# Moving the turned sequences and the dense convolutions among the stages that run beside a scan

## The chip, the cores and the metric

One core of a Trainium2 chip runs the whole program in one launch. The engines are PE (TensorE: matmuls and, as PEld, their weight loads), DVE (VectorE), ACT (ScalarE), POOL (GpSimd) and SP (SyncE, which here issues every DMA). Each engine takes its instructions in the order in which the program gives them, so an instruction that waits holds back what stands behind it on the same engine. The metric is the device time of the launch in microseconds (us), the median of several runs. Beside it stands one execution under the hardware profiler, from which all durations below are taken.

## What is computed

Eight images of 64 x 64 positions with 192 channels pass through two layers. Cut to what matters, the second layer of the reference is

```
y = conv3x3(bn(xl)); y = conv3x3(relu(bn(y)))          # dense convolutions, 96 channels
xl_out = relu(conv1x1(relu(bn(y))))
xi = silu(depthwise3x3(in_proj(ln(xr))))               # 192 channels
xs4 = [x_hw, x_wh, flip(x_hw), flip(x_wh)]             # rows first, and turned: columns first
h = exp(d_t * A) * h + (d_t * u_t) * b_t;  y_t = h . c_t   # the scan, 4096 steps, 4 directions, 16 states
yv = ys[0] + flip(ys[2]) + turned back(ys[1] + flip(ys[3])) + D * xs4
xr_out = out_proj(ln(yv) * silu(z))
out = interleave(xl_out, xr_out) + x
```

The first layer is of the same family: a projection, a depthwise convolution, a state-space pass in chunks that is done with matmuls, and an MLP. The second layer's scan has no such form here and runs as true scans on DVE.

## The kernel before

The second layer's scan is the backbone. An image's scan is cut into 384 units (8 stretches of 1024 steps, 3 tiles of channels, 16 units in a tile), 3072 in all. In each unit SP fetches a tile `dA` (`fetch`, 6 units ahead), ACT takes its exponential (`decay`, L1450, 2 units ahead), PE spreads the input into `dB` (`spread`, L1458, one unit ahead), DVE weighs it (L1473) and scans it (L1480), POOL multiplies by C (L1482), and PE gathers the states of four units (L1500). A unit of the scan has two halves, and in each half the loop calls `beside.half()`.

`Beside` holds a list of stages: Python generators which, each time they are advanced, emit a few instructions and yield a cost, or None for "no more in this half". Each half adds a credit, `rate`, and takes stages' costs from it. `spread_over` sets `rate` when an image begins, from the sum of the stages' costs and the number of halves; a stage that has run in full once (`finish` in front of the first scan) is known by what it yielded, `conv_branch` and `scan_outputs` by numbers written out by hand. What is left when the next image's scan is about to begin, at unit 360 of 384, is emitted at one go by `beside.finish()`. The new image's stages begin at unit 362.

While image b - 1 is scanned, the stages for image b and for the scan of image b - 2 run, in this order:

- `conv0`, `ssd`, `mlp0`: the first layer of image b, whose output is `x1[b]`
- `conv_branch(b - 2)`: the dense convolutions (L895), with `scan_sums(b - 2)` as its side: the sum of the four directions
- `scan_outputs(b - 2)`: normalisation, gate and output projection
- `scan_inputs(b)`: normalisation, projection and depthwise convolution, which writes the sequences `us[b]`
- `transposed(b)`: reads the sequences back in quarters (`whole<-u`, L1114), turns each quarter on ACT into a tile `part` (L1124) and stores it (L1132)

A side is advanced by `cx.aside()` once in each half, up to its next None, in addition to the stage it belongs to; what it yields as cost is ignored. Stages 0 run alone in front of the first scan. During the last image's scan only `conv_branch(6)` with the sums of image 6, `scan_outputs(6)` and `conv_branch(7)` are left, and the sums and outputs of image 7 follow behind the scan (the tail).

SBUF for each stage comes from pools that are opened and closed like a stack; `us`, `ys` and `xns` lie in DRAM, each image's at an address of its own. Matmul results of side work rotate through four PSUM banks (`cx.one`).

Of the kernel before, what the change touches and what calls it, by code (L numbers as in the profile page):

```python
# [1 line left out]

# [7 lines left out]
F32 = mybir.dt.float32  # L10
# [6 lines left out]
HH = WW = 64  # L17
L = HH * WW
PW = WW + 2
C = 192  # L20
CH = C // 2
# [30 lines left out]
def wh(ap):  # L52

    return ap.rearrange("p (h w) -> p w h", h=HH)


def wh_to_hw(ap):

    return ap.rearrange("p (w h) -> p h w", w=WW)
# [16 lines left out]
class Shared:  # L76
# [5 lines left out]
    def __init__(self, tc):  # L82
        self.tc, self.nc, self.pin = tc, tc.nc, tc.keep_in_program_order
        self.k = {}
        self.singles = []
        self.side = None

    def one(self, name):

        self.singles.append(self.singles.pop(0))  # L90
        return self.singles[-1].tile([128, 512], F32, tag="n", name=name)

    def aside(self):

        for piece in self.side or ():
            if piece is None:
                return True
        self.side = None
        return False

# [189 lines left out]
def pause(n):  # L290

    for i in range(n):
        yield None
# [810 lines left out]
def transposed(cx, u):  # L1104

    nc, pin = cx.nc, cx.pin
    with cx.pool("t1") as tp:
        wholes = []
        for n, src in enumerate((u[0], u[2][0:64])):
            wholes.append(tp.tile([src.shape[0], L], F32, tag=f"whole{n}", name=f"whole{n}"))  # L1110

        def load(n, q):
            here = slice(q * L // 4, (q + 1) * L // 4)
            pin(nc.sync.dma_start(out=wholes[n][:, here], in_=(u[0], u[2][0:64])[n][:, here]))  # L1114

        for q in range(4):
            load(0, q)
            yield from pause(1 if q < 3 else 2)
        front = []
        for whole, dst in zip(wholes, (u[1], u[2][64:128])):  # L1120
            for q in range(4):
                w0 = q * WW // 4
                part = tp.tile([whole.shape[0], L // 4], F32, tag="part", name="part", bufs=4)
                pin(nc.scalar.copy(part.rearrange("p (w h) -> p w h", h=HH), wh(whole)[:, w0 : w0 + WW // 4, :]))  # L1124
                front.append((dst[:, q * L // 4 : (q + 1) * L // 4], part))
                if whole is wholes[0]:
                    load(1, q)
                if q % 2 == 1:
                    yield 1.0
                    yield None  # L1130
                if len(front) == 2:
                    pin(nc.sync.dma_start(out=front[0][0], in_=front.pop(0)[1]))  # L1132
        pin(nc.sync.dma_start(out=front[0][0], in_=front.pop(0)[1]))


def scan_sums(cx, y, u):

    nc, pin, k = cx.nc, cx.pin, cx.k

    def slots(n):  # L1140
        for i in range(n):
            yield 1.0
            yield None

    def cols(r, n):
        return slice(r * n, (r + 1) * n)

    with cx.pool("t2") as tp:

        for size, firsts, seconds, v, skip, eye in (  # L1150
            (128, [p[0] for p in y], [p[1] for p in y], u[0], k["skip_a"], k["ident"]),
            (64, [p[2][0:64] for p in y], [p[2][64:128] for p in y], u[2][0:64], k["skip_b"], k["twice"]),
        ):
            whole = tp.tile([128, L], F32, tag="whole", name="whole")
            for q in range(4):
                here = cols(q, L // 4)
                pin(nc.sync.dma_start(out=whole[:size, here], in_=seconds[0][:, here]))
                if size < 128:
                    pin(nc.sync.dma_start(out=whole[size:, here], in_=seconds[1][:, here]))
                yield from slots(1)  # L1160
            if size < 128:
                yield from slots(1)
            else:
                others = []
                for q in range(NB + 1):
                    if q < NB:
                        others.append(tp.tile([128, 512], F32, tag="p1", name="p1", bufs=2))
                        pin(nc.sync.dma_start(out=others[q], in_=seconds[1][:, cols(q, 512)]))
                    yield from slots(3 if q == 0 else 1)
                    if q > 0:  # L1170
                        here = cols(q - 1, 512)
                        pin(nc.gpsimd.tensor_add(whole[:, here], whole[:, here], others[q - 1]))

            def load(r):
                part = tp.tile([128, 512], F32, tag="part", name="part", bufs=3)
                pin(nc.sync.dma_start(out=part[:size], in_=firsts[0][:, cols(r, 512)]))
                vt = tp.tile([size, 512], F32, tag="vt", name="vt", bufs=2)
                pin(nc.sync.dma_start(out=vt, in_=v[:, cols(r, 512)]))
                if size < 128:
                    pin(nc.sync.dma_start(out=part[size:], in_=firsts[1][:, cols(r, 512)]))  # L1180
                    return part, [(eye, part), (skip, vt)]
                p1 = tp.tile([128, 512], F32, tag="p1", name="p1", bufs=2)
                pin(nc.sync.dma_start(out=p1, in_=firsts[1][:, cols(r, 512)]))
                return part, [(eye, part), (eye, p1), (skip, vt)]

            coming = load(0)
            yield from slots(4)
            for r in range(NB):
                (part, terms), coming = coming, load(r + 1) if r + 1 < NB else None
                yield from slots(1)  # L1190
                ps = cx.one("ps_sum")[:size]
                for i, (w, t) in enumerate(terms):
                    pin(nc.tensor.matmul(ps, lhsT=w, rhs=t, start=i == 0, stop=False))  # L1193
                rows = wh_to_hw(whole)[:, r * RB : (r + 1) * RB, :]
                pin(nc.tensor.matmul(ps.rearrange("p (h w) -> p h w", w=WW), lhsT=eye, rhs=rows, start=False, stop=True))
                yield 0.6 * len(terms)
                yield None
                pin(nc.scalar.copy(part[:size], ps))
                yield from slots(1)
                pin(nc.sync.dma_start(out=firsts[0][:, cols(r, 512)], in_=part[:size]))  # L1200
# [72 lines left out]
class Beside:  # L1273
# [14 lines left out]
    def half(self):  # L1288

        self.cx.aside()  # L1290
        self.credit = min(self.credit, self.rate) + self.rate
        while self.credit > 0.0 and self.stages:
            for cost in self.stages[0]:
                if cost is None:
                    return
                self.credit -= cost
                if self.credit <= 0.0:
                    return
            self.stages.pop(0)
# [287 lines left out]
def vision_mamba_pair_kernel(ctx: ExitStack, tc: tile.TileContext, x: bass.AP, p0: dict, p1: dict, out: bass.AP):  # L1587

    B = x.shape[0]
    cx = Shared(tc)  # L1590
# [3 lines left out]
    x1 = dp.tile([B, C, L], F32, tag="x1", name="x1")  # L1594
    cx.singles = [ctx.enter_context(tc.tile_pool(name="ps", bufs=4, space=PSUM))]
    setup(cx, cp, dp, p0, p1)
    us, ys, xns = {}, {}, {}

    def short(b):

        return x1[b].rearrange("(i g) l -> g i l", g=2)

    def sums(b):
        return scan_sums(cx, ys[b], us[b])

    def outputs(b):
        return scan_outputs(cx, ys[b][0], xns[b], short(b)[1], out[b][1])

    def branch(b, side=None):
        return conv_branch(cx, x1[b][0:CH], short(b)[0], out[b][0], side)  # L1610

    def stages(b):

        if b < B:
            us[b] = [d2.tile([128, L], F32, tag=f"u{t}", name=f"u{t}") for t in range(3)]
            ys[b] = [[d2.tile([128, L], F32, tag=f"y{g}{t}", name=f"y{g}{t}") for t in range(3)] for g in range(2)]
            xns[b] = d2.tile([CH, L], F32, tag="xn", name="xn")
            beside.add(conv0(cx, x[b]))
            beside.add(ssd(cx))
            beside.add(mlp0(cx, x[b], x1[b]))  # L1620
        if b > 1:
            beside.add(branch(b - 2, sums(b - 2)))
            beside.add(outputs(b - 2))
        if b == B:
            beside.add(branch(b - 1))
        if b < B:
            beside.add(scan_inputs(cx, x1[b][CH:C], xns[b], us[b]))
            beside.add(transposed(cx, us[b]))

    beside = Beside(cx)  # L1630
    with tc.tile_pool(name="ps_a", bufs=4, space=PSUM) as more:
        cx.singles.append(more)
        stages(0)
        beside.finish()
        beside.costs.update(conv_branch=190.0, scan_outputs=78.0)
        cx.singles.remove(more)

    def tail():
# [100 lines left out]
```

## Time and profile before

| what | us |
|---|---|
| median of 3 runs | 16441.98 (16431.81 to 16492.6) |
| profiled execution: span | 16436.7 |
| in front of the first scan unit | 902.0 |
| scan of image 0 | 1792.5 |
| scans of images 1 to 6 | 1970.2, 1989.4, 1983.3, 2000.9, 1984.0, 1983.7 |
| scan of image 7 | 1589.2 |
| behind the last scan | 241.6 |
| busy: PE, DVE, ACT, POOL | 13372.1, 12230.0, 10412.7, 10527.5 |

The times of the scans are differences between starts of the first L1480 of each image. A scan and its weighing take DVE 2344 ns and 1216 ns, 3.6 us together, so a scan that nothing holds up lasts 384 x 3.6 = 1382 us. No engine is busy all the time: the share of PE is 81% over the span, of DVE 74%, and the DMA engines' is 78.5%. Which of them sets the pace changes from stage to stage, and a share over the span does not tell it. That is why the prediction reads the profile by stages: from the unit in which a stage's first instruction is emitted to the unit of its last.

### The profile page before, as it was taken

How to read it: one execution, taken by the hardware profiler on the slowest of the kernel's cores; microseconds unless marked ns; L12 is line 12 of the kernel's file. 1: busy time of each engine (PE TensorE's matmuls, PEld its weight loads, DVE VectorE, ACT ScalarE, POOL GpSimd, SP SyncE). 2: the span in 40 equal slices, each digit the busy share in tenths (PEclk: the TensorE clock that was granted, in tenths of full speed). 3: DMA queues.
4: the chain of work that ended last, by engine and by line, in shares of the span. 5: the costliest groups of instructions: out<-in, count | busy, mean ns of one | idle time of the engine just before them, and what ended most of it. 6: DMA issues, size and time to landing. Idle time of an engine off the chain costs nothing.

```text
span 16436.7 us, 210821 instructions
## 1 busy us (share of the span) xinstructions
PE 13372.1 (81%) x69608; PEld 4636.5 (28%) x69608; DVE 12230.0 (74%) x9264; ACT 10412.7 (63%) x20023; POOL 10527.5 (64%) x5766
## 2 busy tenths in 40 slices
PE   8977887788877897878888788777898788878876
PEld 4423322332223321333223332233322333211111
DVE  2178887886878767887678876788767886778994
ACT  4466677665775757757576575766657666655654
POOL 3158766775668656686567765677656775566773
PEclk9987888789887897878888798887988779877766
DMA  3288888788887888878888778887778877888885
GB/s 89 84 218 195 210 205 225 190 204 208 204 219 187 205 205 207 209 191 204 208 208 207 198 196 198 217 205 197 204 193 221 198 202 205 193 227 200 211 204 137
DMA packets 1602582, 3241.31 MB, mean 197 GB/s; under 512 B 390152, under 2 KB 841368, under 8 KB 1601496
## 3 DMA queue, kind: packets, MB, share of 16 engines
q1 hardware_dynamic: 1601496, 3227.83, 78.5%
q8 instruction: 559, 9.16, 0.3%
q14 instruction: 527, 4.32, 0.1%
HBM read 2548.91 MB, written 678.18 MB: 196 GB/s over the span
## 4 chain that ended last, share of the span: by engine, by line
PE 30%; DMA 16%; DVE 14%; ACT 13%; POOL 7%; issue 5%; SPq 2%; DVEq 0%; ACTq 0%; POOLq 0%
DVE h L1480 9%; DMA dA<-dld 5%; PE acc L1500 5%; DVE dB L1473 4%; PE ps_c L895 4%; PE ps_cv L343 3%; POOL h L1482 3%; ACT dA L1450 3%; PE dB L1458 2%; DMA dus<-dud 2%; PE ps_sum L1193 1%; ACT L107 1%; PE ps_m L799 1%; PE ps_y L696 1%; ACT h L830 1%
## 5 line engine op out<-in xcount | busy, mean ns | idle before, releaser
L1482 POOL TENSOR_TENSOR h<-h,bc 128x1023 f32<-128x1023 f32 x3072 | 7228.8, 2354 | 4585.2 <-DVE h L1480 3895.8
L1480 DVE TENSOR_TENSOR_SCAN h<-dA,carry,dB 128x1024 f32<-128x1024 f32 x3072 | 7200.8, 2344 | 820.7 <-ACT dA L1450 257.6
L1473 DVE TENSOR_TENSOR dB<-dB,bc 128x1024 f32<-128x1024 f32 x3072 | 3736.3, 1216 | 1827.5 <-PE dB L1458 1823.9
L1450 ACT ACTIVATE dA<-dA,neg_a 128x1024 f32<-128x1024 f32 x3072 | 3512.9, 1144 | 29.3 <-DMA dA<-dld 24.1
L1500 PE MATMUL acc<-h,gather 128*32 128x512 f32 x12288 | 2364.1, 730 | 596.5 <-ACT h L1489 329.0
L1458 PE MATMUL dB<-dus,spread 24*128 24x512 bf16 x6144 | 1370.2, 435 | 664.5 <-DVE h L1480 620.1
L1505 ACT COPY y<-acc 128x512 f32<-128x512 f32 x1536 | 884.8, 576 | 750.3 <-PE acc L1500 677.4
L895 PE MATMUL ps_c<-p,conv_w 96*96 96x512 f32 x2304 | 1287.7, 685 | 37.9 <-ACT p L915 26.9
L1488 ACT COPY carry<-h 128x1 f32<-128x1 f32 x3072 | 584.2, 190 | 856.9 <-DVE h L1480 854.4
L1458 PEld LDWEIGHTS <-spread 24*128 24x128 bf16 x6144 | 308.0, 93 | 2837.2 <-issue 1395.5
L1489 ACT ACTIVATE h<-h,bc 128x1 f32<-128x1 f32 x3072 | 905.2, 295 | 143.3 <-ACT carry L1488 1.8
L696 PE MATMUL ps_y<-X,M 64*64 64x64 f32 x12288 | 605.6, 270 | 418.6 <-issue 232.7
L624 ACT ACTIVATE M<-ps_d,ln_dt 128x64 f32<-128x64 f32 x3072 | 669.1, 335 | 314.6 <-PE ps_d L630 304.6
L343 PE MATMUL ps_cv<-pad,diag 64*64 64x512 f32 x6912 | 841.0, 605 | 7.1 <-ACT y L1505 5.1
L1500 PEld LDWEIGHTS acc<-h,gather 128*32 128x32 f32 x12288 | 311.2, 117 | 1636.3 <-issue 1040.1
L107 ACT ACT_TABLE_LOAD x577 | 740.3, 1283 | 10.0
L696 PEld LDWEIGHTS ps_y<-X,M 64*64 64x64 f32 x12288 | 548.8, 180 | 606.5 <-issue 275.5
L629 PE MATMUL ps_d<-R,after 128*128 128x384 f32 x1024 | 606.4, 685 | 31.2 <-ACT bc L618 14.6
L895 PEld LDWEIGHTS ps_c<-p,conv_w 96*96 96x96 f32 x2304 | 372.6, 180 | 785.5 <-issue 725.4
L618 ACT COPY bc<-ps_t 64x256 f32<-64x256 f32 x256 | 93.4, 365 | 716.7 <-PE ps_t L613 716.5
L373 PE MATMUL ps_h<-oa,w1a 128*128 128x256 f32 x1536 | 484.0, 438 | 76.6 <-ACT y L1505 32.2
L1370 PE MATMUL ps_xp<-u,xp 128*108 128x512 f32 x768 | 470.0, 699 | 92.5 <-DMA u<-u 76.0
(243 smaller groups left out, 18412.4 us busy)
## 6 DMA issues: line engine op xcount, KB each, us to landing
dA<-dld SPq DMA_DIRECT2D x3072, 512.0 KB
dud<-terms SPq DMA_DIRECT2D x192, 768.0 KB
dus<-dud SPq DMA_DIRECT2D x2304, 64.0 KB
bc<-bcd SPq DMA_DIRECT2D x256, 512.0 KB
y<-yrows SPq DMA_DIRECT2D x256, 384.0 KB
u<-u SPq DMA_DIRECT2D x192, 512.0 KB
dld<-dl SPq DMA_DIRECT2D x192, 512.0 KB
y<-y SPq DMA_DIRECT2D x3072, 32.0 KB
```

Source lines behind the costliest of these rows:

```text
L107: self.pin(self.nc.scalar.preload_act_table_set("natural_log_exp_and_others"))
L343: pin(nc.tensor.matmul(ps[64 * b : 64 * (b + 1)].rearrange("p (h w) -> p h w", w=WW), lhsT=diag[:, t, :], rhs=pad[64 * i : 64 * (i + 1), b ...
L696: pin(nc.tensor.matmul(psy[d][here, h * HP : (h + 1) * HP], lhsT=M[here, d, h, :], rhs=X[here, d, h, :], start=True, stop=True,))
L895: pin(nc.tensor.matmul(ps.rearrange("p (h w) -> p h w", w=WW), lhsT=w[:, t, :], rhs=pad[:, dy : dy + RB, dx : dx + WW], start=t == 0, stop ...
L1450: pin(nc.scalar.activation(dAs[q], dAs[q], AF.Exp, scale=k["neg_a"][:, steps[m][1], t, i : i + 1]))
L1458: pin(nc.tensor.matmul(dBs[q][:, half, :], lhsT=k["spread"][at : at + 3 * UD, :], rhs=du_of[n][at : at + 3 * UD, i // 2, :], start=True, s ...
L1473: pin(nc.vector.tensor_mul(dBs[q], dBs[q], of(q)[0]))
L1480: pin(nc.vector.tensor_tensor_scan(order(h, g), order(dA, g), order(dB, g), carry, ALU.mult, ALU.add))
L1482: pin(nc.gpsimd.tensor_mul(h[:, rest], h[:, rest], C_[:, rest]))
L1489: pin(nc.scalar.activation(end, end, AF.Identity, scale=C_[:, last : last + 1]))
L1500: pin(nc.tensor.matmul(ps[32 * v : 32 * (v + 1)], lhsT=k["gather"], rhs=hs[q - 3 + v][:, here], start=True, stop=True))
L1505: pin(nc.scalar.copy(y[:, here], ps))
```

## The change

Three things are changed. `transposed(b)` is no longer a stage of its own behind `scan_inputs`: it becomes the front part of the side of `conv_branch`, ahead of the sums, and `scan_inputs(b)` moves in front of that branch. Side work's costs are added up in `cx.spent` and taken from the credit, and the written-out costs of `conv_branch` and `scan_sums` change. And the dense convolutions of image 5 leave the scan of image 6, which now has the turned sequences and the sums as stages of their own, for the scan of image 7, which has three dense convolutions. Inside `transposed` the two source tiles share one slot, so that the second tile's loads follow the first tile's copies; the pauses are longer (a copy in every second half), and `part` has 3 buffers in place of 4.

```diff
     def aside(self):
         for piece in self.side or ():
             if piece is None:
                 return True
+            self.spent += piece
         self.side = None
         return False
...
     with cx.pool("t1") as tp:
         wholes = []
-        for n, src in enumerate((u[0], u[2][0:64])):
-            wholes.append(tp.tile([src.shape[0], L], F32, tag=f"whole{n}", name=f"whole{n}"))
+
+        def whole():
+            wholes.append(tp.tile([(128, 64)[len(wholes)], L], F32, tag="whole", name="whole"))
...
-        for q in range(4):
-            load(0, q)
-            yield from pause(1 if q < 3 else 2)
         front = []
-        for whole, dst in zip(wholes, (u[1], u[2][64:128])):
+        for n, dst in enumerate((u[1], u[2][64:128])):
+            whole()
+            for q in range(4):
+                load(n, q)
+                yield from pause(1 if q < 3 else 3)
             for q in range(4):
                 w0 = q * WW // 4
-                part = tp.tile([whole.shape[0], L // 4], F32, tag="part", name="part", bufs=4)
-                pin(nc.scalar.copy(part.rearrange("p (w h) -> p w h", h=HH), wh(whole)[:, w0 : w0 + WW // 4, :]))
+                part = tp.tile([wholes[n].shape[0], L // 4], F32, tag="part", name="part", bufs=3)
+                pin(nc.scalar.copy(part.rearrange("p (w h) -> p w h", h=HH), wh(wholes[n])[:, w0 : w0 + WW // 4, :]))
                 front.append((dst[:, q * L // 4 : (q + 1) * L // 4], part))
-                if whole is wholes[0]:
-                    load(1, q)
-                if q % 2 == 1:
-                    yield 1.0
-                    yield None
+                yield from pause(2)
                 if len(front) == 2:
                     pin(nc.sync.dma_start(out=front[0][0], in_=front.pop(0)[1]))
...
     def slots(n):
-        for i in range(n):
-            yield 1.0
-            yield None
+        return pause(n)
...
-                yield 0.6 * len(terms)
+                yield 1.1 * (len(terms) + 1)
                 yield None
...
         self.cx.aside()
-        self.credit = min(self.credit, self.rate) + self.rate
+        self.credit = min(self.credit, self.rate) + self.rate - self.cx.spent
+        self.cx.spent = 0.0
...
+        turned = []
+        if b < B:
+            beside.add(scan_inputs(cx, x1[b][CH:C], xns[b], us[b]))
+            turned = [transposed(cx, us[b])]
+        if 1 < b < B - 1:
+            beside.add(branch(b - 2, itertools.chain(*turned, sums(b - 2))))
+        else:
+            for gen in turned:
+                beside.add(gen)
+        if b == B - 1:
+            beside.add(sums(b - 2))
+        if b == B:
+            beside.add(branch(b - 3, sums(b - 2)))
         if b > 1:
-            beside.add(branch(b - 2, sums(b - 2)))
             beside.add(outputs(b - 2))
         if b == B:
+            beside.add(branch(b - 2))
             beside.add(branch(b - 1))
-        if b < B:
-            beside.add(scan_inputs(cx, x1[b][CH:C], xns[b], us[b]))
-            beside.add(transposed(cx, us[b]))
...
-        beside.costs.update(conv_branch=190.0, scan_outputs=78.0)
+        beside.costs.update(conv_branch=250.0, scan_outputs=78.0, scan_sums=60.0)
```

## The prediction

> **What bounds the kernel now.** I read the stages of one full interval first (the busy time of each engine in windows; image 3's scan, from the emission of conv0 to that of the next conv0), then the last image, then the stalls inside a stage.
>
> ```profile
> core 0: us, PE busy (x) PEld busy (x) DVE busy (x) ACT busy (x) POOL busy (x), PEclk, DMA share, GB/s
> 6552.00:6866.00 314.00, 274.21 (x1930) 103.10 (x1928) 255.35 (x147) 230.99 (x427) 205.17 (x103) 0.92 0.89 221
> 6866.00:7397.00 531.00, 397.47 (x3202) 171.32 (x3203) 436.40 (x437) 306.27 (x807) 427.69 (x281) 0.74 0.76 187
> 7397.00:7850.00 453.00, 378.18 (x1682) 157.61 (x1681) 343.60 (x245) 333.28 (x549) 276.01 (x124) 0.90 0.79 199
> 7850.00:8147.00 297.00, 283.07 (x771) 77.66 (x772) 192.17 (x110) 143.01 (x262) 168.10 (x92) 0.93 0.85 219
> 8147.00:8304.00 157.00, 126.83 (x283) 28.08 (x282) 113.44 (x91) 118.18 (x188) 94.22 (x50) 0.71 0.74 176
> 8304.00:8474.00 170.00, 160.88 (x762) 39.43 (x762) 150.22 (x98) 132.62 (x226) 114.03 (x60) 0.91 0.87 218
> 8474.00:8508.00 34.00, 9.71 (x36) 1.30 (x33) 17.55 (x11) 18.86 (x23) 15.59 (x7) 0.63 0.94 268
> 8508.00:8537.00 29.00, 13.18 (x39) 2.01 (x40) 17.91 (x11) 21.57 (x31) 15.12 (x7) 0.50 0.83 244
> ```
>
> These are conv0, ssd, mlp0, the branch (dense convolutions with the sums), outputs, scan inputs, turned, and a rest without side work. In the program's order they cover 73, 91.5, 89, 54.5, 25.5, 40.5, 4.5 and 5.5 units. The branch is PE's: 283 of 297 us, 5.4 us a unit, while DVE (3.6 us a unit) idles a third of it. Turned is nobody's: no engine is over 60%.
>
> ```profile
> 8483.80 0.20 ACT L1488 COPY carry<-h 128x1 f32<-128x1 f32 x1
> 8484.09 0.30 ACT L1489 ACTIVATE h<-h,bc 128x1 f32<-128x1 f32 x1
> 8496.82 3.73 ACT L1124 COPY part<-whole 128x1024 f32<-128x1024 f32 x2 [12.44 <-DMA whole<-u]
> ...
> 8501.68 2.35 DVE L1480 TENSOR_TENSOR_SCAN h<-dA,carry,dB 128x1024 f32<-128x1024 f32 x1 [13.07 <-ACT dA L1450]
> ```
>
> The timeline of ACT (three lines) and DVE (one) there: the copy waits 12.44 us for quarters asked for just before, the decays stand behind it on ACT, and DVE's scan loses 13.07 us.
>
> The last image's windows: branch with sums, outputs, branch, nothing beside, and behind the scan its sums and its outputs.
>
> ```profile
> 14620.00:15152.00 532.00, 444.62 (x1167) 102.39 (x1161) 406.34 (x233) 276.06 (x504) 341.75 (x167) 0.75 0.85 213
> 15152.00:15389.00 237.00, 186.55 (x462) 38.68 (x460) 202.87 (x143) 174.73 (x289) 164.93 (x81) 0.66 0.87 210
> 15389.00:15862.00 473.00, 387.48 (x1096) 88.12 (x1094) 419.00 (x241) 278.72 (x505) 338.14 (x161) 0.76 0.87 205
> 15862.00:16195.00 333.00, 178.82 (x584) 26.66 (x584) 319.86 (x185) 190.08 (x352) 248.75 (x109) 0.62 0.81 194
> 16195.00:16327.00 132.00, 78.83 (x124) 18.41 (x122) 0.08 (x1) 10.96 (x20) 12.38 (x9) 0.75 0.50 145
> 16327.00:16437.00 110.00, 98.83 (x128) 23.39 (x128) 25.43 (x40) 61.77 (x80) 19.83 (x16) 0.66 0.26 71
> ```
>
> They cover 116, 51.5, 120 and 92.5 units. Alone, the scan is DVE's, 3.6 us a unit, and moves 333 x 194 / 92.5 = 0.70 MB a unit.
>
> **The change, by intervals.** No matmul, scan or copy is added; stages get other numbers of units. The built order of the changed kernel gives, in images 1 to 5: conv0 70, ssd 92, mlp0 84.5, scan inputs 37.5, branch with turned and sums 72, outputs 24.5, rest 3.5. A stage's time at another count I take from two counts of the same stage. Image 0's windows (346 us for 86.5 units of conv0, 560 for 102 of ssd, 493 for 104.5 of mlp0, 194 for 48.5 of scan inputs) and the last image's outputs give slopes of 2.4, 2.8, 2.6, 3.0 and 3.1 us a unit.
>
> Images 1 to 5, each: -3 x 2.4 + 0.5 x 2.8 - 4.5 x 2.6 - 3 x 3.0 - 1 x 3.1 = -30. Turned and the rest took 34 + 29 = 63 for 10 units, and 3.5 x 3.6 = 13 stay: -50. The branch grows from 54.5 to 72 units. From below it is PE's work: the gather and spread matmuls there are 39.8 + 21.7 us, with the projections 1.2 us a unit, so 283 + 17.5 x 1.2 = 304, at the present 95% 320. From above, the line through 297 (54.5 units) and 532 (116) gives 364. A third number is the DMA's: 297 us x 219 GB/s = 65 MB, 17.5 x 0.70 = 12 more, and 6 for the turned sequences (3 in, 3 out), 83 MB; at 232 GB/s, the most that a long window shows (conv0 of image 0, share 0.92), 358, at the 268 of the turned window 310. I take 345, between PE's number and the DMA's: +48. The eight turned copies (1.91 us each on ACT) now stand a unit apart, their first one three halves (7 us) behind its last quarter's load, not at once, and `decay` is two units ahead; SP also issues the 8 loads and 8 stores past the `dA` fetches, which are 6 units ahead (20 us of cover). I leave +5 of their waits, between 0 and the present 12.4. Together -27, five times: **-135** (bounds -57 and -1 each).
>
> Image 0: turned gets 14 units, rest 2.5; before it was 32 + 59 us for 18. 16.5 units are 59 at 3.6; by the DMA 16.5 x 0.70 + 6 = 18 MB at 232, 76. I take 72, and +4 for 1.5 units more ahead of it: **-15**.
>
> Image 6 has no branch: conv0 81, ssd 96.5, mlp0 97.5, scan inputs 46, turned 14, sums 42 units, 5 units of outputs, and at unit 360 nearly all of outputs (by the costs it yields, 64.8 of 76.8) is emitted at one go, ahead of everything of the scan on every engine. By the slopes 333 + 545 + 475 + 187. Turned 62 (50 by the scan, 68 by 16 MB at 232). The sums move 18.9 MB (their DMA rows' counts by their sizes), with the scan's 42 x 0.70 it is 48 MB: 207 at 232, 179 at 268; 190. Then 18, and the burst: the tail's outputs took 110, 0.84 of that is 92, less where PE is warm (60 at least); 80. Then 7 of rest. Sum 1897, against 1985: **-88** (-145 to -53).
>
> Image 7: branch with sums at 93 units: 444 on the line, 347 by PE at the clock of images 1 to 6; 425. Outputs at 33.5: 157 + 8 x 3.1 = 182. Two branches at 69 units: scan's floor 248; PE at this image's clock (207.8 us of convolutions and 1.36 a unit in the window of 120) 302, over 0.95 318; 285 each. 115.5 bare units: 416. With 14 in front 1607 against 1589: **+18** (-134 with both lower ends, to +103).
>
> Here the clock decides. Rows: PEclk is 0.93 where PE is busy 95%, 0.76 at 82%, 0.62 at 54%, so a denser branch gets a value between the first two. The Trainium skill (TensorE: Matmul & The Clock Gate, The HAM clock gate) says that half speed is the idle state and some 3.4 us of sustained work lifts it; by it alone the two branches fall to the scan's 248 each and image 7 to 1533. The Trainium skill (DMA: Bandwidth & Descriptors, Where 436 GB/s comes from) puts a core's HBM limit near 358 GB/s, by which the branch's 83 MB are 232 us and never bind; the rows show no long stretch over 232 GB/s, at a share of 0.92.
>
> In front: the second tile's loads now wait for the first's copies and slot, and the scan's first load of that tensor behind them: one load's wait, seen there as 11.09 us: **+10**. The tail is as it was.
>
> Sum: +10 - 15 - 135 - 88 + 18 = -210; span 16436.7 - 210 = 16227, and the median stands 5 above that span: **16232, said as 16230**.
>
> **The rivals.**
> - *More than that* (0.17): the DMA keeps up and PE gets its clock. Branch 320 and no copy waits, -57 x 5 = -285; image 6 -130, image 7 -50, ends -5: -470, 15,970. For it: 268 GB/s was moved for 34 us. Against: only for 34 us.
> - *The work is only moved* (0.15): the branch stays on the line (364, -8 x 5 = -40), image 6 -53, image 7 +103, ends -5: +5, 16,447. For it: the row of 116 units lost 116 us on a scan-bound 416 although PE was at 84%.
> - *Slower: ACT waits for each turned quarter* (0.12). 7 x 8 copies; if each still waits 8 us (12.4 less one unit's spacing) with the decays behind it, 56 x 8 = 448 on top of -210: 16,680. It decides from 210 / 56 = 3.75 us a copy. For it: the row of 12.44 passed whole to DVE, `part` has a buffer less, its store has one unit to land. Against: the loads were six in 4 us then.
> - *It does not do what it says* (0.03): excluded by the order for the place of the copies, open for my reading of the credit.
>
> **How the numbers follow.** The forecast holds 0.53. A measurement tells from no change about 0.5%, 82 us. Faster: 0.51 of the forecast, 0.17, and 0.03 of the moved case, 0.71. Same: 0.02 of the forecast, 0.09 of the moved case, 0.03 of the last: 0.14. Slower: 0.03 of the moved case and 0.12: 0.15. The likeliest's own bounds are 16,080 to 16,370; the range reaches on to 16,040 and 16,440.
>
> **What would show it.** Right: scans of images 1 to 5 near 1955, of image 6 near 1895, of image 7 near 1607; no scan gap of 12 us from `dA` at the turned copies; a block of outputs without scans near unit 360 of image 6; branch windows with PE under 95% and DMA over 0.88. Wrong: turned copies that wait over 4 us each, or branches in image 7 still at a clock of 0.75.

## The result, and the profile after

| | us |
|---|---|
| before, median of 12 runs | 16446.24 (16394.84 to 16492.6) |
| changed, median of 12 runs | 16517.78 (16494.99 to 16567.97) |
| ratio, 95% interval | 1.0043 [1.003, 1.0057] |
| profiled execution of the changed kernel: span | 16508.1 (before 16436.7) |

The forecast was 16,230. The changed kernel is 0.4% slower instead of 1.3% faster. In the profiled executions, part by part (the scan of an image is again the time between two first L1480):

| part | before | after | change | predicted |
|---|---|---|---|---|
| in front | 902 | 910 | +8 | +10 |
| image 0 | 1792 | 1820 | +27 | -15 |
| images 1 to 5, sum | 9928 | 9970 | +42 | -135 |
| image 6 | 1984 | 1965 | -19 | -88 |
| image 7 | 1589 | 1613 | +24 | +18 |
| tail | 242 | 231 | -11 | 0 |
| span | 16437 | 16508 | +71 | -210 |

The same windows as before, image 3's scan in the changed kernel: conv0, ssd, mlp0, scan inputs, the branch with turned and sums, outputs.

```profile
core 0: us, PE busy (x) PEld busy (x) DVE busy (x) ACT busy (x) POOL busy (x), PEclk, DMA share, GB/s
6614.00:6922.00 308.00, 270.66 (x1904) 101.11 (x1904) 245.36 (x141) 220.65 (x406) 197.70 (x99) 0.92 0.86 217
6922.00:7469.00 547.00, 414.50 (x3218) 175.80 (x3218) 439.60 (x441) 311.24 (x816) 430.33 (x282) 0.72 0.76 184
7469.00:7898.00 429.00, 361.65 (x1664) 154.46 (x1656) 326.55 (x233) 310.50 (x521) 258.32 (x116) 0.89 0.80 201
7898.00:8061.00 163.00, 149.20 (x730) 36.31 (x730) 141.16 (x93) 127.53 (x217) 110.73 (x58) 0.91 0.84 211
8061.00:8445.00 384.00, 318.57 (x888) 83.67 (x886) 253.28 (x145) 199.67 (x345) 218.30 (x113) 0.88 0.90 226
8445.00:8592.00 147.00, 112.28 (x285) 26.30 (x284) 109.40 (x89) 117.19 (x183) 90.10 (x48) 0.81 0.75 183
```

Read the fifth row against the branch of before: there PE was busy 283 of 297 us and the DMA engines 85%; here PE is busy 319 of 384, and the DMA engines 90% at 226 GB/s. PE, which set the branch's pace before, now idles 65 us of it. The second row is the other surprise: ssd has half a unit more than before (92 and 91.5) and takes 16 us more, at a clock of 0.72 where it was 0.74. As means over images 1 to 5, units and us:

| stage | before | after | predicted change |
|---|---|---|---|
| conv0 | 73, 315 | 70, 311 | -7 |
| ssd | 91.5, 527 | 92, 547 | +1 |
| mlp0 | 89, 453 | 84.5, 427 | -12 |
| scan inputs | 40.5, 172 | 37.5, 165 | -9 |
| outputs | 25.5, 157 | 24.5, 151 | -3 |
| branch (after: with turned) | 54.5, 301 | 72, 381 | +48, +5 for copies |
| turned and rest | 10, 60 | 3.5, 12 | -50 |

The 48 us that turned and the rest gave up came nearly as forecast (50). The branch took 80 for them.

The last image of the changed kernel: branch 5 with sums, outputs, branch 6, branch 7.

```profile
14679.00:15116.00 437.00, 351.62 (x1026) 88.90 (x1020) 324.19 (x186) 222.35 (x409) 276.93 (x139) 0.87 0.88 221
15116.00:15288.00 172.00, 145.73 (x357) 32.45 (x354) 140.97 (x108) 140.62 (x225) 114.19 (x59) 0.74 0.80 198
15288.00:15582.00 294.00, 245.99 (x739) 66.27 (x738) 240.64 (x139) 167.24 (x305) 201.60 (x103) 0.85 0.82 199
15582.00:15854.00 272.00, 237.78 (x760) 63.86 (x758) 241.84 (x140) 166.79 (x305) 206.13 (x105) 0.96 0.85 216
```

These came within 13 us of what was worked out, in both directions (437 for 425, 172 for 182, 294 and 272 for 285 each). The two branches alone ran at clocks of 0.85 and 0.96, no longer at 0.76.

Image 6 of the changed kernel, its windows for turned, the sums, and the start of the outputs:

```profile
14173.00:14243.00 70.00, 31.83 (x84) 4.35 (x84) 49.19 (x30) 42.50 (x60) 39.88 (x18) 0.55 0.90 220
14243.00:14471.00 228.00, 146.58 (x393) 30.25 (x392) 147.83 (x85) 101.78 (x189) 124.64 (x58) 0.74 0.90 232
14471.00:14534.00 63.00, 57.53 (x98) 13.65 (x98) 28.84 (x31) 43.06 (x61) 25.75 (x15) 0.73 0.55 142
```

Turned and the sums are both at a DMA share of 0.90, and no engine is busy more than 70% of either: as stages of their own they wait for transfers. In the 228 us of the sums PE waited 33.8 us for the sums' tile `part`. The block of outputs at unit 360 shows on the timeline of DVE, whose lines give start and duration:

```profile
14494.14 2.33 DVE L1480 TENSOR_TENSOR_SCAN h<-dA,carry,dB 128x1024 f32<-128x1024 f32 x1
...
14572.95 1.22 DVE L1473 TENSOR_TENSOR dB<-dB,bc 128x1024 f32<-128x1024 f32 x1
14574.20 2.35 DVE L1480 TENSOR_TENSOR_SCAN h<-dA,carry,dB 128x1024 f32<-128x1024 f32 x1
```

Between two scans lie 80.1 us, the forecast's 80.

The turned copies stand on ACT's timeline inside the branch (L1124 of before is L1129 here), and the line of DVE shows the scan that stands behind the fourth of them:

```profile
8100.07 1.99 ACT L1129 COPY part<-whole 128x1024 f32<-128x1024 f32 x1 [11.11 <-DMA whole<-u]
8103.42 1.95 ACT L1129 COPY part<-whole 128x1024 f32<-128x1024 f32 x1
8107.68 1.97 ACT L1129 COPY part<-whole 128x1024 f32<-128x1024 f32 x1
8117.55 1.91 ACT L1129 COPY part<-whole 128x1024 f32<-128x1024 f32 x1 [5.47 <-DMA u<-part]
```
```profile
8120.60 2.35 DVE L1480 TENSOR_TENSOR_SCAN h<-dA,carry,dB 128x1024 f32<-128x1024 f32 x1 [6.08 <-ACT dA L1450]
```

All eight copies of this image waited 20.5 us on ACT, 2.6 us each: the wait that the slower rival feared (8 each) is small, and the scan behind the fourth copy lost 6 us to it. What PE waited for inside the branch (total, times, longest):

```profile
PE ps_sum L1192 <- DMA part<-y: 16.6, 4, 14.3
PE acc L1500 <- POOL h L1482: 10.5, 1, 10.5
PE ps_c L898 <- ACT p L918: 10.0, 2, 8.1
```

Before, the first of these was 3.0 us (as means over images 1 to 5, 5.2 before and 19.6 here). The load of `part` is asked for a fixed number of halves ahead of its matmul, and what fills these halves on PE has changed: in the stretch from the first to the last matmul of the sums, the dense convolutions (tile `ps_c`) are 148 matmuls before and 64 in the changed kernel. The first row is before, the second the changed kernel:

```profile
core 0: us, PE busy (x) PEld busy (x) ACT busy (x), PEclk, DMA share, GB/s
7919.00:8089.00 170.00, 71.02 (x148) 22.30 (x148) 10.03 (x16) 0.98 0.89 231
8209.00:8368.00 159.00, 32.22 (x64) 9.17 (x64) 5.06 (x8) 0.89 0.93 232
```

The cost of the sums is now taken from the credit, so fewer convolutions run beside them. The experiments tell whether this makes the loads late, or the turned sequences in the same queue.

### The profile page after: what moved, and what is told of

Same layout as the page of the kernel before. It is cut to its first block, busy times and chain, and to the rows that moved or that the text cites. A ratio compares the mean times of both kernels' runs of the same rounds, so it can differ in the third digit from the quotient of the medians.

```text
span 16508.1 us, 210904 instructions
## 1 busy us (share of the span) xinstructions
PE 13316.7 (81%) x69608; PEld 4635.0 (28%) x69608; DVE 12235.0 (74%) x9264; ACT 10356.3 (63%) x19977; POOL 10532.1 (64%) x5766
## 5 line engine op out<-in xcount | busy, mean ns | idle before, releaser
L1480 DVE TENSOR_TENSOR_SCAN h<-dA,carry,dB 128x1024 f32<-128x1024 f32 x3072 | 7200.7, 2344 | 716.8 <-ACT carry L1488 304.5
L1500 PE MATMUL acc<-h,gather 128*32 128x512 f32 x12288 | 2310.1, 725 | 549.6 <-ACT h L1489 165.2
L898 PE MATMUL ps_c<-p,conv_w 96*96 96x512 f32 x2304 | 1213.7, 657 | 71.4 <-ACT p L918 68.7
```

Source lines behind the costliest of these rows:

```text
L1480: pin(nc.vector.tensor_tensor_scan(order(h, g), order(dA, g), order(dB, g), carry, ALU.mult, ALU.add))
L1500: pin(nc.tensor.matmul(ps[32 * v : 32 * (v + 1)], lhsT=k["gather"], rhs=hs[q - 3 + v][:, here], start=True, stop=True))
```

## The experiments

Three parts make the change: turned in the side (with the new order), the counting, and image 5's branch moved. Ratios are to the kernel before, measured on the same chip, with 95% intervals. Each build also has its own `rate` beside images 1 to 5. By the formula of `spread_over` it is 2.204 before, 2.178 in the two builds below without counting, 2.289 with counting alone, and 2.262 in the changed kernel and with image 5's branch back.

### The parts one by one

The change without the counting:

```diff
-            self.spent += piece
-        beside.costs.update(conv_branch=250.0, ...
+        beside.costs.update(conv_branch=190.0, ...
```

> The change without its counting: side work's costs are not taken from the credit, and the dense convolutions' cost is 190 again. The branch with the turned sequences and the sums then covers 55 units instead of 72. Theory 1 (the branch is limited by the DMA, 226 GB/s at a share of 0.90 in the changed kernel): its bytes fall by 17 x 0.70 = 12 MB to some 73 MB, so it takes about 320 us instead of 380, the other stages get the difference back, scans of images 1 to 5 near 1983, total 16,470 (1.001 to 1.003 of before). Theory 2 (ACT's waits for the turned copies set the branch): with less time between loads and copies the waits grow, branch 350 or more, total over 16,600. Theory 3 (counting alone makes it slower): back to 16,440 or below.

Measured: 1.0094 [1.0067, 1.0121]. The branch has 55 units and 335 us, at 221 to 223 GB/s and a DMA share of 0.84 to 0.86; ssd has 93.5 and 556, the scan inputs 190 us for 41.5 units. None of the three theories came out whole: the branch lies between the 320 of the first and the 350 of the second, the total (16600.6) is that of the second, and without counting the kernel is slower, not faster, as against the third. PE's wait for `part` in the branch is 6.7 us in image 3, and 1.3 as the mean of images 1 to 5, although the turned sequences share the queue:

```profile
PE ps_sum L1191 <- DMA part<-y: 6.7, 1, 6.7
```

The change with image 5's branch back in image 6's scan:

```diff
-        if 1 < b < B - 1:
+        if 1 < b < B:
             beside.add(branch(b - 2, itertools.chain(*turned, sums(b - 2))))
...
-        if b == B - 1:
-            beside.add(sums(b - 2))
         if b == B:
-            beside.add(branch(b - 3, sums(b - 2)))
+            beside.add(branch(b - 2, sums(b - 2)))
...
-            beside.add(branch(b - 2))
             beside.add(branch(b - 1))
```

> The change without its third part: image 5's dense convolutions run beside image 6's scan again. All theories: the scan of image 6 becomes like images 1 to 5 (1990, from 1965), that of image 7 falls to about 1580 (from 1613), so the total is that of the change within 30 us. If the block of outputs at unit 360 of image 6 cost 80 us for nothing, the total falls by 60 or more.

Measured: 1.0023 [1.0007, 1.0039]; image 6 1979, image 7 1564. By the ratios this is 0.2% (33 us) below the change, about as expected and not the 60 us of a block that costs 80 us for nothing. The intervals overlap: moving image 5's branch brought nothing and may have cost 0.2%.

Turned in the side only, uncounted and image 5 where it was (both edits above):

> Only the first part: turned sequences in the side of the dense convolutions, side work not counted, image 5 where it was. Theory 1 (DMA): the 50 us saved behind the scan inputs come back in the branch as 6 MB at 226 GB/s = 27 us and in the stages after it, scans of images 1 to 6 about 1975 to 1985, total within 40 us of before. Theory 2 (ACT's waits): branch 350 or more, scans over 2010, total over 16,600.

Measured: 1.0089 [1.0068, 1.0111]; branch 55 units, 335 us, scans of images 1 to 6 between 2003 and 2021. The total is 150 us above the kernel before, not within 40, and the branch is below the 350 of theory 2: neither came out.

Counting only, with the order and `transposed` of before:

> Only the second part: side work counted (cost 250), the sequences turned in their own stage at the end, image 5 where it was. The branch covers 68.5 units with the sums alone. Theory 1 (DMA): 65 + 14 x 0.70 = 75 MB at 226 GB/s are 331 us, PE's work 316: some 335; scans of images 1 to 6 about 1985 to 1995, total within 60 us of before. Theory 3 (counting alone makes it slower): total like the change, 16,510 or more.

Measured: 1.0037 [1.0021, 1.0052]; branch 68.5 units, 348 us; ssd 92.5, 547. The total, 63 us above before, lies at the edge of both theories (within 60, or 16,510 and more). Here the turned sequences are not in the branch, and still PE waits for `part` (image 3; the mean of images 1 to 5 is 25.5 us):

```profile
PE ps_sum L1194 <- DMA part<-y: 25.9, 5, 10.4
```

So the sums' late loads come with the counting, not with the turned sequences: 25.5 us with counting alone, 1.3 and 3.3 us with the turned sequences in the side and no counting.

As totals, turned alone is +0.9%, counting alone +0.4%, both +0.2%, with the move +0.4%: no build gains. These cannot be read as the price of each part, because the builds differ in `rate` too, and the rate alone moves the kernel by as much (below).

### What the branch waits for

All turned transfers, but no copies on ACT: the store takes its quarter from `whole` itself, so that the second sequence is not turned.

```diff
-                pin(nc.scalar.copy(part.rearrange(...), wh(wholes[n])[:, w0 : w0 + WW // 4, :]))
-                front.append((dst[:, ...], part))
+                front.append((dst[:, ...], wholes[n][:, q * L // 4 : (q + 1) * L // 4]))
                 yield from pause(2)
-                if len(front) == 2:
+                while len(front) > 1 or (q == 3 and front):
                     pin(nc.sync.dma_start(out=front[0][0], in_=front.pop(0)[1]))
-        pin(nc.sync.dma_start(out=front[0][0], in_=front.pop(0)[1]))
```

> The change with all DMAs of the turned sequences but without ACT's copies: the quarters are stored as they were loaded, so the turned scans work on sequences in the wrong order. Theory 1 (the DMA limits the branch): branch of images 1 to 5 stays at 370 to 380 us. Theory 2 (ACT's copies and their waits cost): it falls by 20 to 35 us, scans of images 1 to 5 to 1965.

Measured: 1.0055 [1.0035, 1.0075]. The branch stays at 72 units and 381 us. The copies cost nothing there; the slower rival is out.

No turned sequences for images 2 to 7; their scans read image 1's:

```diff
-            turned = [transposed(cx, us[b])]
+            turned = [transposed(cx, us[b])] if b < 2 else []
...
-    selective_scan(cx, lambda b: us[b], ...
+    selective_scan(cx, lambda b: [us[b][0], us[min(b, 1)][1], us[min(b, 1)][2]], ...
```

> The change without the turned sequences of images 2 to 7, loads, copies and stores: the turned scans read image 1's. The branch still covers 72 units. Theory 1 (DMA): 6 MB less at 226 GB/s, branch 350 to 355 us; the rest as with no_copies. Theory 2 (ACT's copies): the same 350 to 355, but then no_copies has it too. If neither bounds it (PE's clock and the waits of the sums alone), the branch stays over 370.

Measured: 0.9928 [0.9902, 0.9954], branch 72 units and 356 us (mean). Its window in image 3:

```profile
8004.00:8358.00 354.00, 311.13 (x889) 83.96 (x890) 252.97 (x145) 185.29 (x337) 218.30 (x113) 0.89 0.89 227
```

In image 3, 354 x 227 = 80.4 MB were moved, against 384 x 226 = 86.8 MB in the changed kernel. The copies alone gave nothing, so the 25 us between 381 and 356 belong to the 6 MB of transfers. Whether their bytes cost this or their 16 places in SP's queue was not separated. Two things are not equal here: the sums begin 14 units earlier in the branch, and PE still waits 14.0 us for `part`.

The change with the sums' matmuls one half later behind their loads, so that each block of the sums also takes one half more:

```diff
                 (part, terms), coming = coming, load(r + 1) if r + 1 < NB else None
-                yield from slots(1)
+                yield from slots(2)
```

> The change with one half more between a block's loads in the sums and its matmuls (4 halves in place of 3). If PE's waits for part<-y in the branch (17 to 22 us an image) come from loads that are asked for too late, they fall to under 8 us and the branch of images 1 to 5 from 381 to 360 to 368. If the DMA's rate limits the branch, it stays at 375 to 385 and its rate at 226 GB/s. (Image 6's sums then reach into the block at unit 360; only images 1 to 5 are compared.)

Measured: 1.0008 [0.9996, 1.0021], branch 72 units and 367 us. The window in image 3, and PE's wait for `part` in it:

```profile
8036.00:8408.00 372.00, 314.96 (x890) 82.19 (x886) 253.13 (x144) 199.56 (x345) 218.04 (x113) 0.91 0.91 232
```
```profile
PE ps_sum L1192 <- DMA part<-y: 1.6, 2, 1.5
```

The wait went from 16.6 to 1.6 and the branch from 381 to 367, as expected if the loads are asked for too late: 14 us an image were the late loads. The other case, a limit at 226 GB/s, is out: the same bytes went through faster. In image 1 the branch moved them at 242 GB/s:

```profile
4071.00:4429.00 358.00, 312.20 (x890) 82.72 (x886) 252.76 (x144) 199.44 (x345) 218.12 (x113) 0.92 0.92 242
```

Over the five images it was 231 to 242 GB/s, at a share of 0.91 to 0.92, so neither 226 nor 232 GB/s is a ceiling of the branch.

### Image 0 and the value of `rate`

In the changed kernel `transposed` only pauses where it yielded a cost of 1.0 four times, and so, known by what it yielded in front, it counts 0 where it counted 4. With that, `rate` in image 0 is 1.912 instead of 1.918. The windows of the scan inputs there, in the changed kernel, and in the change with the 4 put back:

```diff
-        beside.costs.update(conv_branch=250.0, scan_outputs=78.0, scan_sums=60.0)
+        beside.costs.update(conv_branch=250.0, scan_outputs=78.0, scan_sums=60.0, transposed=4.0)
```

> The change, with a cost of 4 written out for the turned sequences, as they had before: the rate beside image 0's scan is 1.918 again instead of 1.912, everything from image 1 to 5 is untouched. Theory A (the rate's value itself matters: it sets which instructions of a stage meet in a half, and with it PE's granted clock): image 0's scan inputs fall from 223 us to 195 with their depthwise matmuls from 705 ns to about 630, total 25 us less than the change. Theory B (the slower stage comes from what the change does in image 0): it stays at 220.

```profile
2329.00:2552.00 223.00, 201.07 (x819) 46.28 (x818) 180.92 (x115) 153.99 (x264) 139.99 (x70) 0.78 0.77 197
```
```profile
2321.00:2520.00 199.00, 180.20 (x816) 42.21 (x816) 180.04 (x115) 153.88 (x263) 140.35 (x71) 0.85 0.87 223
```

The second row is the experiment's. The same matmuls fill 49 units in both, and PE is busy 201 us at a clock of 0.78 or 180 at 0.85. Image 0 fell from 1820 to 1790. In total it is 1.0036 [1.0018, 1.0055], which overlaps the change's interval. The stage itself leaves no doubt: in the profiled executions of the nine kernels with a rate of 1.912 these scan inputs took 216 to 223 us, in those of the eight with 1.918 they took 195 to 200, two with the change's `transposed` among them. So the third digit of a credit costs image 0's scan inputs 25 us.

The same on the kernel before: only the written-out cost of `conv_branch`, 190 there, is changed.

```diff
-        beside.costs.update(conv_branch=190.0, scan_outputs=78.0)
+        beside.costs.update(conv_branch=184.0, scan_outputs=78.0)
```

> The kernel before, with 184 for 190 as the cost of the dense convolutions and nothing else: the rate beside images 1 to 6 is 2.196 instead of 2.204, ssd covers 94 units instead of 91.5. Theory A (the rate's value matters): ssd takes 545 to 560 us as in every changed kernel so far, instead of 527, scans of images 1 to 6 some 15 to 30 us longer, total 16,500 to 16,600. Theory B (the rate matters only through the number of units, 2.5 x 2.8 = 7 us a scan in ssd, given back by the other stages): total within 30 us of before.

> The same with 200: rate 2.218, ssd 92 units. Theory A: ssd away from 527 by over 10 us, total 16,470 or more. Theory B: ssd 527 to 530, total within 30 us of before.

> The kernel before with 215 for 190 as the cost of the dense convolutions: rate 2.240 beside images 1 to 6. By straight lines through the stages' times (theory B) the 6 units that become free at the end cost 6 x (3.6 - 2.7) = 5 us a scan: total within 60 us of before. Theory A (the rate's value matters by which instructions meet): ssd 540 to 550 instead of 527 at the same 91.5 units, scans 1990 to 2010, total 16,480 to 16,580.

And on the change, in place of 250:

> The change with conv_branch written out as 240 in place of 250, nothing else: rate 2.248 in place of 2.262 in images 1 to 5, 1.792 in place of 1.836 in image 7. Straight lines (my prediction's way): every stage gets 0.6% more units (conv0 70.5, ssd 92.5, mlp0 85, scan inputs 37.5, branch 72.5), the rest loses two units; by the slopes of 2.4 to 3.1 us a unit that is under 3 us an image, 16,500 to 16,540 in all. The rate's own value decides: the same units, but ssd, mlp0, scan inputs and conv0 of images 1 to 5 move by 10 to 30 us a stage, their scans by 10 us or more each, and the total by 50 us or more in a direction that neither theory can tell.

> The change with conv_branch written out as 260: rate 2.276 in images 1 to 5, 1.879 in image 7. Straight lines: every stage 0.6% fewer units, two more in the rest, under 3 us an image, 16,500 to 16,540, and 240 and 260 lie on two sides of 16,518 or all three within 30 us. The rate's own value decides: 50 us or more from 16,518, and the three costs 240, 250, 260 need not be in order; where the change's mean over the three lies against the four costs of the kernel before (184, 190, 200, 215: 16,549, 16,446, 16,343, 16,601) then tells whether the change itself does anything.

| kernel | cost | rate, images 1 to 5 | ratio | ssd: units, us |
|---|---|---|---|---|
| before | 184 | 2.196 | 1.0075 [1.005, 1.01] | 94, 546 |
| before | 190 | 2.204 | 1 | 91.5, 527 |
| before | 200 | 2.218 | 0.9956 [0.9942, 0.9969] | 92, 524 |
| before | 215 | 2.240 | 1.011 [1.0095, 1.0126] | 91.5, 554 |
| change | 240 | 2.248 | 1.0144 [1.012, 1.0168] | 92, 555 |
| change | 250 | 2.262 | 1.0043 [1.003, 1.0057] | 92, 547 |
| change | 260 | 2.276 | 1.0059 [1.0043, 1.0075] | 92.5, 547 |

Only the rates 2.204 and 2.218 have ssd under 530 us; at the other five it takes 546 to 555. The kernel before thus stood at a rate that suits ssd, and the changed kernel did not.

ssd's window in image 3, with cost 200 and then with cost 215:

```profile
6846.00:7373.00 527.00, 398.86 (x3202) 171.76 (x3202) 437.56 (x438) 307.32 (x813) 428.81 (x282) 0.74 0.79 189
```
```profile
6940.00:7498.00 558.00, 416.31 (x3215) 173.10 (x3212) 438.06 (x441) 310.61 (x815) 430.62 (x282) 0.71 0.74 180
```

The same DVE and POOL work and nearly the same matmuls take 527 or 558 us, PE's own busy time 399 or 416. At 184 and 215 theory A (the rate's value matters) came out. At 200 neither did: ssd stayed as it was and the total fell by 73 us. The costs 240, 250 and 260 do not lie in order either, and straight lines would have them within 30 us of each other: they span 1%, although 260 by itself (16538.77) is where the lines put it. The change at 240, image 3: mlp0, scan inputs, branch, outputs.

```profile
7522.00:7966.00 444.00, 369.07 (x1678) 156.71 (x1670) 336.25 (x239) 324.26 (x538) 266.22 (x120) 0.88 0.79 197
7966.00:8135.00 169.00, 159.12 (x720) 38.14 (x722) 139.30 (x92) 124.66 (x211) 109.76 (x58) 0.84 0.79 200
8135.00:8530.00 395.00, 320.99 (x888) 84.11 (x888) 253.32 (x145) 199.83 (x346) 216.00 (x112) 0.86 0.86 223
8530.00:8680.00 150.00, 139.84 (x274) 30.04 (x272) 102.79 (x85) 110.44 (x172) 83.32 (x44) 0.60 0.67 164
```

Against the changed kernel, the branch is 11 us longer with as many instructions, at a share of 0.86; the outputs keep PE busy 140 us instead of 112, at a clock of 0.60 instead of 0.81. Why one spacing suits the scan's own pattern and another does not is not settled by these runs. A lower clock and a lower DMA share go with the slow ones, and either can be the cause or the consequence.

### Another place for turned

The kernel before with the turned sequences as the side of the outputs, which come last; the turned sequences go in eighths, an idle step of the outputs is left out, and to fit, `o`, `sh`, `v` and `sq` have fewer buffers. The diff shows the call only. The sum of the costs is held so that the rate is as before (2.204).

```diff
-            beside.add(outputs(b - 2))
+            beside.add(outputs(b - 2, turned(cx, us[b])))
```

> The kernel before with the turned sequences beside scan_outputs, whose windows have the DMA to spare (176 GB/s, share 0.74), and not beside the dense convolutions; order branch with sums, scan inputs, outputs with turned; a written-out cost of 208.56 holds the rate beside images 1 to 6 at 2.204, so conv0, ssd, mlp0 and the branch are as before. To make room scan_outputs has fewer buffers and no idle step. Theory 1 (the DMA limits where the turned sequences lie): the branch stays near 301, turned and the rest fall from 60 us to 10 x 3.6 = 36, outputs go from 157 to 157 to 165: scans of images 1 to 6 about 1965, total 16,310 to 16,380. Theory 2 (turning costs wherever it lies): outputs 180 or more, total 16,430 or more.

A miss: 1.0065 [1.0053, 1.0078]. conv0, ssd, mlp0 and the branch are as before (317, 527, 453, 303), but the scan inputs take 198 for 41 units (172 before, for 40.5), and the outputs 170 for 25, 15 us of it (mean) waiting for the store of the only `o`. The first of these shows, at the same rate, that the order of stages moves a stage that nothing in it touches.

### The parts of the miss undone together

Image 5's branch back, the sums' matmuls one half later, and the 4 for `transposed`, in one kernel:

> The change with image 5's branch back in image 6's scan, the sums' loads one more half ahead of their matmuls, and transposed counted as 4 so that image 0 has the rate of before (1.918); rate 2.262 in images 1 to 6. If the parts add up: five_back's 16,476, less 14 us for each of six branches and 30 us for image 0, 16,360, ratio 0.995 to 0.996; branch 72 units and 365 to 368 us in images 1 to 6, image 0 near 1790. If the branch is the DMA's alone: the later matmuls give nothing in total, 16,445.

Measured: 0.9948 [0.993, 0.9967], 16353.39 us against 16449.34. The branch of image 3:

```profile
7969.00:8342.00 373.00, 325.12 (x890) 85.00 (x886) 253.50 (x146) 199.76 (x345) 218.55 (x113) 0.89 0.89 232
```

The branches of images 1 to 5 take 365 us for 72 units on average, image 0 is 1774, images 1 to 6 1962 to 1980. The three parts add up as expected (16,360). It is faster than the kernel before by about as much as that kernel itself is with cost 200 (0.9956), and the two intervals overlap, so this gain cannot be put down to the order.

## Why the prediction was wrong

The forecast's direction was wrong: it said -210 us on the span, and +71 came, 281 apart. By part: images 1 to 5 +177, image 6 +69, image 0 +42, image 7 +6, in front -2, tail -11. The branch is 5 x 27 = 135 of the 281: with its measured time in the sum, the forecast would still have been -75.

**Images 1 to 5, the step that failed: "I take 345, between PE's number and the DMA's".** The branch took 381, 80 more than before, not 53 with the copies' 5. The three numbers I had were PE's 320, the DMA's 358 and the line's 364, and nothing justified the middle. In its place the runs showed two terms. The turned sequences' transfers take 25 us of the branch (381 without the copies, 356 without the transfers). And the sums' loads come late, 14 us, which I had at nothing: I looked at SP's queue for the turned copies, and not at what the counting does to the sums, whose matmuls now follow their loads with 64 convolution matmuls among them in place of 148. The rest, some 40 us for 17.5 more units if the two add, was not taken apart. The 5 us for copies were not there: without copies the branch was the same.

The DMA's number had two wrong sizes, which partly cancel. I counted 0.70 MB a unit for the scan from the stretch with nothing beside it and came to 83 MB; the windows moved 86 to 87. And 232 GB/s, the most in my windows, is no ceiling: with the loads in time the branch took 367 us as a mean, at up to 242 GB/s. I also called the stage of the turned sequences nobody's; its row has the DMA engines at 0.94.

**The stages' straight lines.** I took every stage's time as a slope on its units. Together the five stages came out near (-23 for -30), but by accident: ssd was +20 for +1, and mlp0 -26 for -12. In image 0 the scan inputs cost 29 more at nearly the same units, where I had put +4 for all stages ahead of turned. The value of the rate was missing from the model, and by itself it moves the kernel by -0.4 to +1.1% of the time (before) and by 1% within the change. This is as large as the whole forecast gain, so the sum's sign was not decided by its terms.

**Image 6.** The sums took 228, not 190: they moved 228 x 232 = 53 MB against the 48 that I counted, I had gone below even my 207, and PE waited 33.8 us for their late loads, a term that I had not. The other stages were 38 over (554 for 545, 489 for 475, 199 for 187, 70 for 62, less 5 in conv0), and the outputs with the block and the rest 97 for 105. The block itself was right, 80.1 for 80.

**Image 7 and the clock.** Image 7 came out at +24 for +18, but from parts that missed by up to 13 us and cancel. The clock of its two branches, 0.85 and 0.96, did rise from 0.76. My reason does not hold, though: of three rows I made a rule from PE's busy share to its clock, and mlp0's row, 0.90 at 83% busy, already broke it; the two branches were busy 84% and 87%. The 1.36 us a unit that I used there leave out the projections, which the branch's 1.2 included; with them it is 1.6.

**What was right.** Turned and the rest gave 48 for 50. In front +8 for +10, in one execution; the other changed kernels with these copies show 905 to 910, those with the order of before 901 to 905. Nothing showed the slower rival: copies waited 2.6 us each, under its own threshold of 3.75. The rival that came nearest is "the work is only moved", 16,447, whose line gave 364 for the branch; it too was too low.

**What stays open.** At three costs the change is slower than the kernel before; but the kernel before at costs 184, 200 and 215 is 0.75% slower, 0.4% faster and 1.1% slower, so no single pair of these says what the order is worth apart from its rate. What the change's parts cost that can be named (late loads, image 0's rate, image 5's move) is named and was taken back in the last experiment. The tail's -11 is no effect of the change: its instructions are the same in both kernels, and in the profiled executions of all builds it took between 230 and 259 us. Why a rate suits a stage is open.

## What to carry to other kernels

Work moved beside a stage is not free because that stage's engine has room: 6 MB of transfers in a stage whose DMA engines were 89% busy without them took 25 us. Where three estimates of a stage stand side by side, the middle needs a reason of its own. When a change thins out the work between a load and its use, look at whether the load still lands in time. When a planner spaces the side work by a credit, run the same kernel at a few neighbouring values first; a gain smaller than the scatter over these values cannot be put down to the order.

## What was not expected of the hardware

PE's busy time for the same matmuls depended on how they were spaced: ssd 399 us at a granted clock of 0.74 and 416 at 0.71, the scan inputs of image 0 180 us at 0.85 and 201 at 0.78. The Trainium skill (TensorE: Matmul & The Clock Gate, The HAM clock gate) gives half speed as the idle state and sustained work as what lifts it. The share of time in which PE is busy was not enough to tell the clock here: in the outputs at cost 240 PE was busy 140 of 150 us at a clock of 0.60, at cost 250 112 of 147 us at 0.81.

The rate of transfer was no fixed ceiling. The branches with 72 units moved 217 to 243 GB/s, and inside one of the changed kernel a stretch of 150 us went at 266 GB/s:

```profile
6120.00:6270.00 150.00, 127.65 (x343) 35.34 (x342) 97.62 (x56) 85.64 (x143) 91.51 (x48) 0.87 0.95 266
```

The Trainium skill (DMA: Bandwidth & Descriptors, Where 436 GB/s comes from) puts a core's limit at HBM near 358 GB/s. The windows shown in this case reach 268 GB/s at most, for 34 us with the DMA engines 0.94 busy.
